# A convolution-attention kernel: the last 18 keys scored once per image, two map tiles in turn, a 1 KB ring of DMA descriptors

## The chip, the cores and the metric

The kernel runs on one core of one Trainium2 chip. Its time is the device time in microseconds (us), the median of several runs. A core has a matrix engine (TensorE, PE in the profile), a vector engine (VectorE, DVE), a scalar engine for activations (ScalarE, ACT), GpSimd (POOL), SyncE (SP), which only issues transfers, and 16 DMA engines. PE's results go to PSUM, where the kernel's tiles take eight banks of 128 partitions by 512 fp32 numbers; its other tiles are in SBUF. All data here is fp32.

## What is computed

The input is `x`, eight images of 256 channels by 32 by 32 pixels. Layer 0 is attention in eight heads of 32 channels, with a query for each of the 1024 pixels. Its keys and values come from four pooled copies of the projected map, 32x32, 16x16, 11x11 and 5x5, each with a depthwise 3x3 convolution added, so there are 1024 + 256 + 121 + 25 = 1426 keys. Layer 1 is attention over the 1024 tokens of an image with one head of 256, and a mixture of eight three-layer networks (the FFN) follows it. Cut to what matters here:

```python
kv = jnp.einsum('bchw,oc->bohw', x, kv_w)
k_map, v_map = kv[:, :C], kv[:, C:]
def pooled(t):                       # ratios 1, 2, 3, 6
    p = jnp.einsum('bchw,ph,qw->bcpq', t, Mh, Mw)
    p = p + _depthwise(p, dconv_w[i], dconv_b[i])
    ...
ks_ = _layernorm(pooled(k_map).transpose(0, 2, 1), norm_w, norm_b)
vs_ = _layernorm(pooled(v_map).transpose(0, 2, 1), norm_w, norm_b)
attn = jax.nn.softmax(jnp.einsum('bhqd,bhkd->bhqk', q_g, k) * SCALE, axis=-1)
out_att = jnp.einsum('bhqk,bhkd->bhqd', attn, v)
```

## The kernel before

**Units and steps.** Layer 0's attention runs in units: an image `b`, a half `c` of the heads (four heads, 32 partitions each) and a half of the queries (512). There are 8 x 2 x 2 = 32 units. The keys are cut in `NKC` = 12 chunks, eleven of 128 and a last one of 1426 - 11 x 128 = 18. A step takes one chunk in one unit, so the loop at L1827 has 384 steps. A step does the following.

- `scores` (L1477): for each of the four heads a product with 32 rows (the head's channels), up to 128 columns (the keys) and 512 moving elements (the queries). Each head has its own 32 rows of the array and its own PSUM bank of the tile `sc`, which is four banks and exists once. One activation then takes exp of all four banks, 128 x 2048 numbers, into a tile `pt`, of which there are six. The last chunk fills 18 partitions only, over the same 2048 numbers.
- `values` (L1487), one step later: four products with the keys as rows and the 32 channels of a head as columns, each into its own 32 partitions of the bank `pv`, added up over the twelve chunks.
- The softmax sums: after every second chunk `add` (L1499) has POOL issue a DMA that adds the newer `pt` onto the older one in SBUF. For the last chunk it adds 18 partitions. `sums` (L1506) adds the six resulting tiles of a unit on VectorE, and a product with ones sums over partitions.

So the products of `scores` use the array in strips of 32 rows, those of `values` in strips of 32 columns, and the rest of the program in one piece or, where `narrow` (L751) says so, in column strips.

**The order.** A planner, class `Flow` (from L656 on), writes the order of every engine's instructions at build time. It has a model of costs (`cost`, L721, and `note`, L761) and a list of generators. Before an instruction is recorded a generator yields what it needs (an engine, tiles that must be ready, a PSUM slot, or a condition `until`). In the gaps of the loop at L1827 `step` (L864) takes up runnable generators as filler: preparing the next image, then layer 1 of earlier images, by rank and with a budget of 4 us (`PACE`) and 2 us (`PACE1`) of PE time per step. `finish` runs generators until a condition holds, such as the next image's keys being there. The order is fixed in the program, and waits on semaphores guard the data.

**Maps.** For each image after the first, `maps` (L1088) projects four maps (two halves of values, then two of keys), each in three slices of up to 512 columns, from PSUM through ScalarE into `p` and into an accumulator `acc` (three of these). `convolve` (L1241) then runs the taps on VectorE (`taps`, L1215). There is one tile `p` (`pmap`, L1128). So a map's first two slices wait until the large taps of the previous map have read it (`read[0] >= len(todo)`), its last slice until all its taps are done, and the number of maps started is held by `len(todo) < 3 + 2 * freed[0]`. The first image (`first_maps`, L1144) uses a slot of `acc` as the `p` of its map 3. `by_tokens` (L1266) transposes finished maps to one key per partition and normalises them; `value_tokens` (L1433) keeps the results as `vts[b][g]`, four chunks in each.

**Descriptors.** [...] whose size can be given where the program is made (L2539); here it is left at its default.

Of the kernel before, what the change touches and what calls it, by code (L numbers as in the profile page):

```python
# [10 lines left out]
AF = mybir.ActivationFunctionType  # L11
# [5 lines left out]
P = 128  # L17
# [5 lines left out]
OFFS = (0, 1024, 1280, 1401)  # L23
NK = 1426
NKC = 12
NE = 8
SCALE0 = DH ** -0.5
SCALE1 = C ** -0.5
# [627 lines left out]
class Flow:  # L656
# [64 lines left out]
    def cost(self, engine, op, out, ins):  # L721
        n = 1
        for s in (out.shape if op != "bn_stats" else ins[0].shape)[1:]:
            n *= s
        if op == "tensor_reduce":
            n = 1
            for s in ins[0].shape[1:]:
                n *= s
        if "dma" in op:
            return 1.0 if engine == "POOL" else 0.4  # L730
        if engine == "PE":
            if op == "transpose":
                return 0.13
            c = max(0.2, 0.00169 * n)
            return c if self.tiling(ins) is None else c / 4
        psum = any(i.space == PSUM for i in ins)
        if engine == "ACT":
            return 0.15 + 0.00084 * n + 0.16 * any(i.free_size() == 1 for i in ins[1:])
        if engine == "POOL":
            if n <= 64 and op == "tensor_tensor":  # L740
                return 0.3 + 0.17 * n if n <= NKC else 0.3
            return 0.15 + (0.0023 if op == "tensor_tensor" else 0.0015) * n
        if op == "scalar_tensor_tensor":
            return 0.23 + 0.00103 * n
        if op == "reciprocal":
            return 0.1 + 0.0064 * n
        if op in ("tensor_scalar", "tensor_copy") and not psum:
            return 0.14 + 0.00065 * n
        return 0.15 + 0.00107 * n
# [5 lines left out]
    @staticmethod  # L755
    def tiling(ins):

        rows, columns = ins[0].shape[0], ins[0].shape[-1]
        return "columns" if columns <= DH and rows > 8 else "rows" if rows == DH else None

    def note(self, engine, op, ins, args, kwargs):  # L761
# [22 lines left out]
        if engine == "PE":  # L784

            tiling = None if op == "transpose" else self.tiling(srcs)
            if tiling != self.tiled:
                cost += {None: 0.2, "rows": 0.2, "columns": 0.13}[tiling]
                self.tiled = tiling

        wide = [a for a in srcs if a.space != PSUM and a.free_size() > 4]
# [103 lines left out]
def attention(tc, kit, f, outer, ended, nb, consts, x, t1, t2, hn, bounds, vecs, q_t, kv_t, proj_t, gqk_t, wqk, wqkv, vecs1, w1_d, w1c, gate_d, wrc, vecs2, bnvec):  # L895
# [6 lines left out]
    with ExitStack() as ctx:  # L902
# [159 lines left out]
            f.ve.tensor_tensor(bias, ps[:, 0:2], vec[:, V_PB : V_PB + 2], ALU.add)  # L1062

        ks, qs, vts = {}, {}, {}
        made = [0]
        turn = [-1]
        todo, done, read, freed, key_parts, normalised = [], [], [4], [0], [0], [0]

        def pe(*tiles, tag=None):
            return "PE", tiles, tag  # L1070
# [7 lines left out]
        def pool(*tiles):  # L1078
            return "POOL", tiles, None

        def until(cond):
            return None, cond, None

# [4 lines left out]
        def maps(xp):  # L1088

            for m in (2, 3, 0, 1):  # L1090
                c = m % 2
                yield until(lambda: read[0] >= len(todo) and len(todo) < 3 + 2 * freed[0])
                p = pmap
                acc = T(work, [P, NK], "acc", bufs=3)
                for s0, w in KEY_SLICES:
                    if s0 >= HW:
                        yield until(lambda: len(done) >= len(todo))
                    src = source(xp, s0, w)
                    yield pe(src, tag="sm")
                    ps = small()  # L1100
                    for k in range(2):
                        f.pe.matmul(
                            ps[:, :w],
                            lhsT=kvw[:, k, m * P : (m + 1) * P],
                            rhs=src[:, k, :],
                            start=k == 0,
                            stop=k == 1,
                        )
                    f.act.activation(p[:, s0 : s0 + w], ps[:, :w], AF.Copy)
                    for s, n in enumerate(SIDES):  # L1110
                        a, z = max(OFFS[s], s0), min(OFFS[s] + n * n, s0 + w)
                        if a < z:
                            f.act.activation(
                                acc[:, a:z],
                                ps[:, a - s0 : z - s0],
                                AF.Identity,
                                bias=db(c, s),
                                scale=mid[:, c * 4 + s : c * 4 + s + 1],
                            )
                todo.append((c, p, acc))  # L1120
# [4 lines left out]
            return dy, dx, max(0, -dy), n - max(0, dy), max(0, -dx), n - max(0, dx)  # L1125


        pmap = T(work, [P, NK], "p")  # L1128
        f.split(pmap, 512, HW)
        first, large, whole, pooled, asked = {}, [], [], [], []  # L1130

        def first_diagonals():
# [11 lines left out]
        def first_maps(xp):  # L1144


            for m in range(4):
                if m < 2:
                    p = T(work, [P, 4, 512], "pt", bufs=6).rearrange("p j q -> p (j q)")
                    acc = T(l1, [P, NK], "v") if m else T(work, [P, NK], "kn", bufs=3)  # L1150
                else:
                    p = T(work, [P, NK], "acc", bufs=3) if m == 3 else pmap
                    acc = T(work, [P, NK], "acc", bufs=3)
                for t in (p, acc):
                    if t is not pmap:
                        f.split(t, 512, HW)
                first[m] = p, acc
            for m, s0 in [(m, s0) for g in (0, 2) for s0 in (0, 512) for m in (g, g + 1)] + [(m, HW) for m in range(4)]:
# [70 lines left out]
        def first_taps():  # L1229
            for m in (2, 3):  # L1230
                yield until(lambda: "maps" in large)
                yield from taps(m - 2, 0, *first[m])
                large.append(("values", m))
            yield until(lambda: whole)
            for m in (2, 3, 0, 1):
                for s in range(1, 4):
                    yield from taps(m % 2, s, *first[m])
                whole.append(m)
            done.extend(first[m][1] for m in (2, 3, 0, 1))
# [193 lines left out]
        def value_tokens(b, g):  # L1433
# [2 lines left out]
            accs = done[4 * b : 4 * b + 2] if b else [first[m][1] for m in (2, 3)]  # L1436
            vt = T(work, [P, 4, C], "vt", bufs=6)
            yield from by_tokens(accs, vt, 4 * g)
            vts[b][g] = vt

        def key_tokens(b, g):
# [45 lines left out]
        def values(b, c, kc, pt, pv):  # L1487
            w = KEY_CHUNKS[kc][1]
            for j in range(4):
# [3 lines left out]
                    lhsT=vts[b][kc // 4][:w, kc % 4, h * DH : (h + 1) * DH],  # L1493
                    rhs=pt[:w, j, :],
                    start=kc == 0,
                    stop=kc == NKC - 1,
                )

        def add(kc, pt, into):  # L1499

# [323 lines left out]
        f.spawn(chain(mix(), weights1(), outputs()), 5)  # L1824
        f.spawn(layer1(), 6)
        f.columns = True
        steps = [(b, c, half, kc) for b in range(nb) for c in range(2) for half in range(2) for kc in range(NKC)]  # L1827

        pts = {}
        for i in range(len(steps) + 1):  # L1830
            if i < len(steps):
# [9 lines left out]
                    f.finish(lambda: {0, 1}.issubset(whole))  # L1841
                if b == 0 and kc == 0:
                    f.finish(lambda: (c, half) in asked)
                pts[i] = scores(b, c, sl, kc)
                f.step()
            if i:
                b1, c1, half1, kc1 = steps[i - 1]
                if kc1 == 0:
                    pv = T(psum, [P, 512], "pv")
                    pairs = []  # L1850
                    sl1 = slice(half1 * 512, half1 * 512 + 512)
                    f.spawn(unit(b1, c1, sl1, i // NKC, pairs), 0)
                f.finish(lambda: kc1 // 4 in vts[b1])
                values(b1, c1, kc1, pts[i - 1], pv)
                if kc1 % 2:
                    add(kc1, pts.pop(i - 1), pts[i - 2])
                    pairs.append(pts.pop(i - 2))
                if kc1 == NKC - 1:
                    f.finish(lambda: projected[0] >= b1)
                    f.act.activation(atts[b1, c1][:, sl1], pv, AF.Copy)  # L1860
            if i < len(steps):
# [688 lines left out]
```

## Time and profile before

| | us |
|---|---|
| median of 3 runs (3305.45 to 3312.34) | 3309.68 |
| the profiled execution's own time | 3310.0 |
| its span, from the first to the last instruction | 3308.1 |
| time outside the span (difference) | 1.9 |
| layer 0's attention loop, from its first exp at 84 to its last at 1956 | 1872 |
| after the loop (rest of layer 1, then the FFN) | 1352 |

The page gives each engine's busy time over the whole span. Since the parts of the program have different limits, the table of stretches matters more, with the span cut where an image's attention starts. Names in the rows are tiles: `sc`, `pv` and `pt` as above, `kn` a half of the keys, `q` the queries, `vt` values by token; `sm` and `sx` are the three PSUM banks of all filler. Nearly every instruction is recorded through one line (L669), so that groups are told apart by their tiles. "32*128" in a row of PE is rows by columns of the array in use. An fp32 product shows as two instructions, so four products are x8.

### The profile page before, as it was taken

The numbers are of one execution on the slowest core, as the hardware profiler recorded it, in microseconds if no ns is written. First come the engines' busy times: TensorE is split into PE (matmuls) and PEld (weight loads), VectorE is DVE, ScalarE is ACT, GpSimd is POOL, SyncE is SP. The second block draws the span as 40 slices with busy tenths as digits, with TensorE's granted clock in tenths as the row PEclk, the third lists the DMA queues.
The fourth block names the chain that finished last, engine by engine and source line by source line (L and its number), as shares of the span: only waits on it lengthen the run. The fifth ranks groups of instructions, "written<-read, shape, count | busy, mean of one in ns | idle before, by whom it ended". The sixth has DMA issues, their size and how long they took to land. (4 is left out here: it accounts for less than half of the span.)

```text
span 3308.1 us, 57168 instructions
## 1 busy us (share of the span) xinstructions
PE 3098.8 (94%) x23038; PEld 1790.7 (54%) x23038; DVE 2455.2 (74%) x4068; ACT 1733.4 (52%) x2330; POOL 1217.1 (37%) x1315
## 2 busy tenths in 40 slices
PE   8687899999999999999899889999999999999997
PEld 4322234334334334334334236767888888888886
DVE  5687688797886887987875455447888787777776
ACT  4476675675676576666666543343333344444442
POOL 2211411412213213213112112007656567777775
PEclk9798999999999999999999999999999999999999
DMA  2357655745646756655556557125434310000000
GB/s 75 84 127 165 131 100 145 147 93 143 142 103 143 147 132 131 132 133 114 125 127 143 122 119 246 60 86 178 153 134 153 139 65 20 20 25 27 20 14 21
DMA packets 110754, 362.70 MB, mean 110 GB/s; under 512 B 13504, under 2 KB 38856, under 8 KB 87248
## 3 DMA queue, kind: packets, MB, share of 16 engines
q0 software_dynamic: 28608, 179.85, 28.2%
q1 hardware_dynamic: 78512, 177.13, 15.5%
q8 instruction: 184, 3.01, 0.4%
q10 hardware_dynamic: 3360, 1.97, 0.2%
q14 instruction: 90, 0.74, 0.1%
HBM read 112.45 MB, written 81.31 MB: 59 GB/s over the span
## 5 line engine op out<-in xcount | busy, mean ns | idle before, releaser
L669 ACT ACTIVATE pt<-sc 128x2048 f32<-128x2048 f32 (+1 forms) x384 | 720.5, 1876 | 298.5 <-PE sc L669 246.5
L669 DVE SCALAR_TENSOR_TENSOR acc<-p,vec,acc 128x225 f32<-128x225 f32 (+7 forms) x928 | 532.7, 580 | 31.3 <-ACT acc L669 6.5
L669 PE MATMUL sc<-q,kn 32*128 32x512 f32 (+1 forms) x3072 | 448.1, 653 | 108.0 <-ACT pt L669 105.8
L669 DVE TENSOR_TENSOR pt<-pt,pt 128x1024 f32<-128x1024 f32 x320 | 384.4, 1244 | 144.3 <-DMA pt<-pt 133.1
L669 POOL DMA_DIRECT2D pt<-pt x192 | 171.4, 894 | 769.3 <-ACT pt L669 592.9
L669 PE MATMUL pv<-pt,vt 128*32 128x512 f32 (+1 forms) x3072 | 420.2, 620 | 0.0
L669 ACT ACTIVATE p1c<-bank 128x256 f32<-128x256 f32 x230 | 87.9, 382 | 565.9 <-PE bank L669 554.3
L669 ACT ACTIVATE h<-h,bnvec 128x512 f32<-128x512 f32 x460 | 348.0, 805 | 63.8 <-DVE h L669 54.7
L669 POOL TENSOR_TENSOR rstd<-rstd,mhalf 128x4 f32<-128x4 f32 (+2 forms) x88 | 108.8, 1237 | 697.7 <-DVE rstd L669 586.3
L669 DVE TENSOR_TENSOR h<-p1c,bank 128x512 f32<-128x512 f32 x230 | 156.7, 681 | 211.6 <-PE bank L669 211.0
L669 PEld LDWEIGHTS sc<-q,kn 32*128 32x128 f32 (+1 forms) x3072 | 116.8, 179 | 320.2 <-ACT pt L669 217.8
L669 POOL TENSOR_TENSOR tm<-h,tm 128x256 f32<-128x256 f32 x210 | 241.8, 1151 | 16.5
L669 DVE TENSOR_TENSOR h<-u,bank 128x256 f32<-128x256 f32 x460 | 234.3, 550 | 7.9
L669 PEld LDWEIGHTS pv<-pt,vt 128*32 128x32 f32 (+1 forms) x3072 | 60.9, 108 | 304.2 <-issue 295.1
L669 POOL TENSOR_TENSOR tm<-h 128x512 f32<-128x512 f32 x105 | 137.9, 1313 | 195.2 <-ACT h L669 194.1
L669 DVE TENSOR_TENSOR h<-h,gate 128x1024 f32<-128x1024 f32 x128 | 203.2, 1588 | 0.5 <-ACT h L669 0.5
L669 PE MATMUL bank<-h,w2e 128*128 128x256 f32 (+1 forms) x604 | 193.3, 448 | 2.8 <-DVE h L669 1.9
L669 PE MATMUL sm<-p,v 128*32 128x256 f32 (+1 forms) x2416 | 192.3, 379 | 0.7 <-ACT p L669 0.7
L669 PE MATMUL y<-t,s3e 128*128 128x256 f32 x768 | 187.0, 379 | 2.2 <-POOL t L669 2.1
L669 PE MATMUL bank<-t,s1e 128*128 128x256 f32 x750 | 183.8, 381 | 3.5 <-DVE h L669 3.5
L669 POOL TENSOR_TENSOR t<-h,t 128x256 f32<-128x256 f32 x216 | 172.9, 800 | 17.0
L669 POOL TENSOR_TENSOR t<-h 128x512 f32<-128x512 f32 x108 | 140.1, 1298 | 105.4 <-DVE h L669 80.0
(315 smaller groups left out, 5448.6 us busy)
## 6 DMA issues: line engine op xcount, KB each, us to landing
pt<-pt POOLq DMA_DIRECT2D x160, 1024.0 KB, 7.5
h<-h SPq DMA_DIRECT2D x118, 512.0 KB, 3.3
xi<-in_x_dram SPq DMA_DIRECT2D x16, 512.0 KB, 6.7
t<-t SPq DMA_DIRECT2D x8, 1024.0 KB, 5.6
res<-t SPq DMA_DIRECT2D x32, 256.0 KB, 4.7
t<-res SPq DMA_DIRECT2D x32, 256.0 KB, 4.6
hn<-res SPq DMA_DIRECT2D x32, 256.0 KB, 4.2
hn<-hn SPq DMA_DIRECT2D x16, 512.0 KB, 4.4
```

Source lines behind the costliest of these rows:

```text
L669: ins = fn(*args, **kwargs)
```

## The change

- The last chunk leaves the step list for three of an image's four units. In the first unit (`c` = 0, `half` = 0), after chunk 7, `tail_scores` makes the scores of the last 32 keys for all four units of the image: sixteen products of 32 rows by 32 columns by 512, product (`u`, `j`) with the rows of head `j` and into the partitions 32`u` of bank `j`. One exp puts them into `ptail`. The loop has 8 x (4 x 11 + 1) = 360 steps.
- Of these 32 keys the first 14 are also in chunk 10. `tail_values`, called in each unit right after the values of chunk 10, takes the 32 rows of its unit from `ptail` and a value tile `vz` that holds zeros for those 14 keys. `vz` (two tiles, by the image's parity, zeroed once on POOL) is filled by four small transfers on SP per image, at the end of `value_tokens` for the last group. `tail_add` adds the 18 rows of `ptail` onto chunk 10's `pt` by a DMA from POOL.
- Two tiles `p` are used in turn, so that `maps` may be one map further ahead (`len(todo) - 1`), and the first map of the second image may be projected before any tile of the first is freed.
- The planner's model gets the price of the new kind of product, and the descriptor ring has 1024 bytes of each partition.

```diff
-        todo, done, read, freed, key_parts, normalised = [], [], [4], [0], [0], [0]
+        todo, done, read, freed, key_parts, normalised = [], [], [2], [0], [0], [0]
...
-                yield until(lambda: read[0] >= len(todo) and len(todo) < 3 + 2 * freed[0])
-                p = pmap
+                yield until(
+                    lambda: read[0] >= len(todo) - 1 and len(todo) < (3 + 2 * max(freed[0], 2) if freed[0] else 5)
+                )
+                p = pmaps[len(todo) % 2]
...
-                        yield until(lambda: len(done) >= len(todo))
+                        yield until(lambda: len(done) >= len(todo) - 1)
...
+            if g == 2:
+                yield sp(vt)
+                for u in range(4):
+                    c = u // 2
+                    f.sp.dma_start(vz[b % 2][DH * (u + 1) - NT : DH * (u + 1), :], vt[:NT, 3, c * P : (c + 1) * P])
...
+        def tail_scores(b):
+            t = T(psum, [P, 4, 512], "sc")
+            for j in range(4):
+                r = slice(DH * j, DH * j + DH)
+                for u in range(4):
+                    c, half = divmod(u, 2)
+                    f.pe.matmul(
+                        t[DH * u : DH * u + DH, j, :],
+                        lhsT=ks[b, c][r, NK - DH :],
+                        rhs=qs[b, c][r, half * 512 : half * 512 + 512],
+                        start=True,
+                        stop=True,
+                    )
+            f.act.activation(ptail, t, AF.Exp, scale=SCALE0)
+
+        def tail_values(b, u, pv):
+            for j in range(4):
+                f.pe.matmul(
+                    pv[DH * j : DH * j + DH, :],
+                    lhsT=vz[b % 2][DH * u : DH * u + DH, DH * j : DH * j + DH],
+                    rhs=ptail[DH * u : DH * u + DH, j, :],
+                    start=False,
+                    stop=True,
+                )
+
+        def tail_add(u, into):
+            rows = slice(DH * (u + 1) - NT, DH * (u + 1))
+            f.pool.dma_start(
+                out=into[:NT].rearrange("p j q -> p (j q)"),
+                in_=ptail[rows].rearrange("p j q -> p (j q)"),
+                accum_op=ALU.add,
+            )
...
-        steps = [(b, c, half, kc) for b in range(nb) for c in range(2) for half in range(2) for kc in range(NKC)]
+        order = [*range(8), NKC - 1, *range(8, NKC - 1)]
+        steps = [
+            (b, c, half, kc)
+            for b in range(nb)
+            for c in range(2)
+            for half in range(2)
+            for kc in order
+            if kc < NKC - 1 or c + half == 0
+        ]
...
-                pts[i] = scores(b, c, sl, kc)
+                if kc == NKC - 1:
+                    f.finish(lambda: key_parts[0] > 3 * b + 2 and (b, 1) in qs and (b or len(asked) == 4))
+                    tail_scores(b)
+                else:
+                    pts[i] = scores(b, c, sl, kc)
...
-                if kc1 == NKC - 1:
+                if kc1 == NKC - 2:
+                    u = 2 * c1 + half1
+                    tail_values(b1, u, pv)
+                    pairs.append(pts.pop(i - 1))
+                    tail_add(u, pairs[-1])
...
-    nc = _bacc.Bacc("TRN2", target_bir_lowering=False, num_devices=1)
+    nc = _bacc.Bacc("TRN2", target_bir_lowering=False, num_devices=1, dynamic_dma_scratch_size=1024)
```

## Prediction

> **What bounds the kernel.** I read the busy times by stretch first, because the page's averages mix an attention loop with an FFN. The stretches are the eight images' turns in the loop (two of them left out), the end of layer 1 and the FFN. Columns: stretch, its length, busy time of PE, PEld, DVE, ACT and POOL with instruction counts, granted clock, DMA share, GB/s.
>
> ```profile
> 84.00:326.00 242.00, 181.95 (x1367) 64.33 (x1370) 185.54 (x382) 146.60 (x171) 45.60 (x55) 0.89 0.56 125
> 326.00:563.00 237.00, 217.04 (x2090) 79.04 (x2083) 183.53 (x317) 154.70 (x186) 58.18 (x68) 0.95 0.60 129
> ...
> 1042.00:1271.00 229.00, 217.64 (x2224) 83.29 (x2220) 193.75 (x329) 152.21 (x185) 58.42 (x65) 0.99 0.62 135
> ...
> 1746.00:1956.00 210.00, 198.85 (x2140) 76.24 (x2140) 103.31 (x143) 124.64 (x128) 38.59 (x44) 0.98 0.64 130
> 1956.00:2010.00 54.00, 40.40 (x152) 23.34 (x144) 18.73 (x21) 10.90 (x21) 14.47 (x33) 0.87 0.62 213
> 2010.00:2240.00 230.00, 229.15 (x896) 163.06 (x895) 114.90 (x210) 86.16 (x147) 17.22 (x23) 0.99 0.31 109
> ```
>
> PE is at 95% in a middle image (217.64 of 229) and at 99.6% after the loop, while DVE stays below 85% and ACT below 68%. So PE bounds the program, and its idle time adds to the end. Only the first image, which has no layer 1 to fill gaps, has PE at 75%. PE's own rows come next, by shape, with exp's two rows (busy us, mean ns of one, idle before).
>
> ```profile
> L669 PE MATMUL sc<-q,kn 32*128 32x512 f32 x2816 | 413.7, 657 | 93.6 <-ACT pt L669 91.5 <-ACT kn L669 0.8
> L669 PE MATMUL pv<-pt,vt 18*32 18x512 f32 x256 | 34.9, 616 | 0.0
> L669 PE MATMUL sc<-q,kn 32*18 32x512 f32 x256 | 34.4, 607 | 14.3 <-ACT pt L669 14.3
> L669 ACT ACTIVATE pt<-sc 128x2048 f32<-128x2048 f32 x352 | 660.8, 1877 | 276.6 <-PE sc L669 225.8 <-DMA pt<-pt 24.7 <-issue 10.1
> L669 ACT ACTIVATE pt<-sc 18x2048 f32<-18x2048 f32 x32 | 59.7, 1866 | 21.9 <-PE sc L669 20.7 <-issue 1.2
> ```
>
> The last chunk's 18 keys cost as much as 128: 34.4 / 32 = 1.075 us of PE per step for scores and 1.866 us of ACT. Last, the order in time on PE in three steps of image 4.
>
> ```profile
> 1121.05 1.14 PE L669 MATMUL sc<-q,kn 32*128 32x512 f32 x8
> 1122.12 1.06 PE L669 MATMUL pv<-pt,vt 128*32 128x512 f32 x8
> 1123.12 0.66 PE L669 MATMUL sm<-con,t 128*128 128x128 f32 x4
> 1124.19 1.14 PE L669 MATMUL sc<-q,kn 32*128 32x512 f32 x8 [0.42 <-ACT pt L669]
> ...
> 1128.46 1.06 PE L669 MATMUL pv<-pt,vt 128*32 128x512 f32 x8
> 1129.35 1.90 PE L669 MATMUL sm<-xi,kvw 128*32 128x512 f32 x16
> ```
>
> A step with little filler lasts 3.14 us (1121.05 to 1124.19). The next scores need the one `sc` tile, so they wait for exp, and PE has about 2 us for `values` and filler. A step with more filler lasts as long as its PE work. Such waits are 93.6 + 14.3 = 107.9 us by the rows, 105.8 of it for exp.
>
> **The sum, part by part.**
>
> *Scores, removed:* 32 groups at 1.075 = **34.4 us** of PE.
>
> *Scores, added:* 8 groups of sixteen products, each on its own 32x32 block. The trace shows neither blocks nor sixteen at once. Its nearest rows are four side by side in row strips (`sc`) and in column strips (`pv`), and both take one group's time. In the group at 1124.19 the first four starts lie 7 ns apart. By the row, a group is 1.07 + 24 more instructions x 0.007 = 1.24 us. [...] The ends are 1.07, all free, and 4 x 1.07 = 4.3, if the four products that share a strip of rows queue. I take 1.24, since strips of either kind do run side by side here: **9.9 us**.
>
> *A rule against the change:* [...] here a new mode comes in. In the trace `pv` followed by work in its own mode takes 0.89 us (1128.46 to 1129.35), before another mode 1.00 (1122.12 to 1123.12), and `sc` before `pv` 1.07. So a change of mode costs 0.11 to 0.18 us. Two steps before had filler, sc, pv, filler, sc, pv, filler: four changes. Now they have filler, sc, pv, tail values, filler: again four. The removed group's 1.075 thus holds about 0.15 that comes back behind chunk 10, in 24 places: **+3.6 us**. If the row's saving stood whole it would be 0; if each of 32 tail values paid two changes of its own, 32 x 0.36 = 11.5.
>
> *Values of the last keys:* as many groups, 32 rows in place of 18, in the same 512-element stream: 34.9 us before and after, 0.
>
> PE's work: -34.4 + 9.9 + 3.6 = **-20.9 us**.
>
> *Waits for exp:* 24 exps go, 24 x 1.87 = 44.9 us of ACT, which does not bound. What counts is PE's idle time before scores, 105.8 / 384 = 0.275 us a step. The order of the changed program's PE queue has about as many loop gaps with under 0.8 us of filler as before (72 to 74), so the waits thin out only with the steps: 24 x 0.275 = **-6.6 us**. Ends: 0, if all wait just as long elsewhere; 24 x 0.447 = 10.7 by the removed row's own idle.
>
> *Filler left behind:* 24 budgets fewer move about 70 us of layer 1 past the loop, counted in that order at 0.46 us per 256 columns. It lands where PE is busy 229.15 of 230 us, so 0. Without that cover, at the loop's 95%, it would cost 3.5.
>
> *Two map tiles:* DVE's tap row waits 31.3 us in all over 928 taps, and DVE is not the bound, so 0. Upside: the second image's first map can fill some of the first image's 60 idle us of PE (242 - 182), at most 5. Downside: its taps delay the first image's keys by as much.
>
> *Moved and added on queues:* SP gets 32 transfers of 18 rows of 512 B. The issue waits for ACT to normalise value chunk 11; behind it in SP's order stand filler loads and stores (`res`, `hn`, `q`, the weights). Values are made before keys, so tail values come many steps later, and a transfer lands in 3 to 5 us by rows such as `hn<-pool` at 3.2. I take 0, at most 1 us for each of 8 images. On POOL the two memsets lie in the start, and accumulating transfers stay 192. The new wait of the sixteen scores is for all keys of the image and both `q`. Chunk 8 already waited for the keys, one step later, and `q` is fetched as the unit begins, over 25 us earlier. Nothing on ACT stands behind it but exp: 0. `ptail` frees `pt` slots (exp waits 24.7 us for them now), which I leave for the upside.
>
> *Ring of 1 KB:* Two rows bear on it.
>
> ```profile
> q0 software_dynamic: 28608, 179.85, 28.2%
> pt<-pt POOLq DMA_DIRECT2D x160, 1024.0 KB, 7.5
> ```
>
> 28608 packets over 192 + 28 transfers and 16 engines are 8 per engine and transfer. A transfer lands in 7.5 us and they are issued every second step (6.3 us at the least), so two or three are under way. [...] so 0.
>
> **Sum:** 3308.1 - 20.9 - 6.6 = 3280.6, with 1.9 outside **3282.5**. The profiled execution (3310.0) is 0.3 over the median shown, so I say **3282 us**, 0.8% less. A measurement of this kernel tells about 0.2% (7 us) from no change.
>
> **Rivals.**
>
> 1. *Each removed step takes its whole period along* (3262, chance 0.17). In the unit with the least filler of each image, and in the first image, steps last 3.1 us and the moved values hide under exp. Ten of the 24 places would then give 3.14 and not 1.2, some 20 us more. For it: units of 45 to 50 us in every image, close to 12 x 3.14 = 38. Against it: filler pushed out must be done elsewhere.
> 2. *Half is given back* (3296, 0.13). A shorter loop lets DVE fall behind with the keys (193.75 of 229 in a middle image), and PE waits at the image's start. For it: 60 idle us in the first image. Against it: in `finish` the planner fills with layer 1.
> 3. *The sixteen products queue in four rounds* (3307, 0.07): 8 x 4.3 = 34.4 takes back all the scores gave, then +3.6 - 6.6. No change that can be told. Against it: four different streams already run at once in `pv`.
> 4. *The ring holds POOL, slower* (3335, 0.06). If each accumulating DMA could only be written once the last had drained, POOL would be held 7.5 us in place of 0.9 by 188 transfers, 1240 us more in a loop of 1872 where it is busy some 440. Then `pt` slots and the small powers on POOL come late. At 0.16 us of PE per transfer the gain is gone; at 0.3 it is 56 us. Against it: the packet count above.
>
> The forecast has 0.55; 0.02 remains for other cases of the planner's order. **Range** 3256 to 3301: it takes in the first two rivals and the bounds of the modes, the waits and the maps. Faster by over 0.2%: forecast, rivals 1 and 2, 0.86; within: 0.07; slower: 0.07.
>
> **What would show it.** Scores of 32*32 in about 1.2 us per group (4.3: rival 3). PE busy near 3078 us. Idle before `sc` on exp near 99. Units 2 to 4 of an image shorter by 1.2 us each (3: rival 1). POOL's issue of `pt<-pt` still at 894 ns (several us: rival 4). The stretch after the loop as dense but some 70 us longer. I am wrong if PE's busy time falls by 20 and the span does not.

## The result, and the profile after

| | before | changed |
|---|---|---|
| median of 12 runs each, on one chip (us) | 3310.87 | 3297.39 |
| ratio, with its 95% interval | 1 | 0.9962 [0.9952, 0.9973] |
| span of the profiled execution (us) | 3308.1 | 3298.6 |
| PE busy (us) | 3098.8 | 3093.2 |
| PE idle, span less busy (us) | 209.3 | 205.4 |
| attention loop, first exp to last (us) | 1872 | 1795 |
| after the loop (us) | 1352 | 1421 |

The change gains 13 us where 28 were forecast. The stretches of the changed kernel come first (columns as in the prediction: stretch, length, busy time of PE, PEld, DVE, ACT and POOL, granted clock, DMA share, GB/s). The rows are the first two images, a middle one, the last, the first 52 us after the loop, and a part of the FFN.

```profile
83.00:322.00 239.00, 186.77 (x1390) 67.36 (x1388) 186.01 (x399) 144.92 (x174) 50.62 (x60) 0.89 0.55 124
322.00:527.00 205.00, 184.40 (x1668) 65.59 (x1668) 181.17 (x303) 144.23 (x172) 66.47 (x75) 1.00 0.67 143
988.00:1221.00 233.00, 215.65 (x2174) 82.75 (x2170) 188.86 (x330) 146.35 (x182) 51.56 (x60) 0.97 0.63 136
1689.00:1878.00 189.00, 182.72 (x2052) 67.81 (x2056) 97.07 (x123) 111.20 (x104) 33.75 (x38) 0.99 0.68 139
1878.00:1930.00 52.00, 35.45 (x133) 18.16 (x126) 24.79 (x37) 8.26 (x16) 16.95 (x37) 0.90 0.70 222
1930.00:2160.00 230.00, 226.07 (x887) 164.26 (x886) 108.41 (x191) 83.48 (x145) 15.82 (x16) 1.00 0.30 103
```

The loop is shorter by 77 us and what follows it longer by 69. PE still bounds both parts: 92.6% in the middle image, 98.3% in the FFN. Next, groups of PE by shape (count, busy us and mean ns of one, idle before and what ended it) of the changed kernel.

```profile
L670 PE MATMUL sc<-q,kn 32*128 32x512 f32 x2816 | 414.6, 659 | 106.7 <-ACT pt L670 104.0 <-ACT kn L670 1.0 <-ACT ptail L670 0.5
...
L670 PE MATMUL bank<-h,w2e 128*128 128x512 f32 x248 | 114.9, 606 | 3.4 <-ACT h L670 3.4
L670 PE MATMUL bank<-h,w2e 128*128 128x256 f32 x388 | 100.6, 380 | 2.5 <-DVE h L670 2.5
...
L670 PE MATMUL pv<-ptail,vz 32*32 32x512 f32 x256 | 35.7, 629 | 0.0
...
L670 PE MATMUL sc<-q,kn 32*32 32x512 f32 x256 | 10.7, 656 | 1.0 <-ACT pt L670 1.0
```

The new scores take 10.7 us for eight groups and replace a row of 34.4. In the order of time (start, duration, group, idle before) the first of these eight groups, the second, and one of the removed groups in the kernel before, each with what PE starts next:

```profile
156.64 2.67 PE L670 MATMUL sc<-q,kn 32*32 32x512 f32 x32
159.25 1.93 PE L670 MATMUL pv<-pt,vt 128*32 128x512 f32 x8
...
360.63 1.16 PE L670 MATMUL sc<-q,kn 32*32 32x512 f32 x32
361.71 1.07 PE L670 MATMUL pv<-pt,vt 128*32 128x512 f32 x8
```

```profile
378.42 1.05 PE L669 MATMUL sc<-q,kn 32*18 32x512 f32 x8 [1.09 <-ACT pt L669]
379.40 1.07 PE L669 MATMUL pv<-pt,vt 128*32 128x512 f32 x8
```

From its start to PE's next, the second group takes 1.08 us, and the first, where the granted clock was 0.50, takes 2.61. The removed group takes 0.98, less than the 1.075 that its row's busy time gives, because the end of a group overlaps the start of the next. Idle time before `sc` on exp was 91.5 + 14.3 before; it is 104.0 + 1.0 now. The same view of the kernel before has, for the FFN's second layers:

```profile
L669 PE MATMUL bank<-h,w2e 128*128 128x256 f32 x420 | 108.6, 380 | 1.9 <-DVE h L669 1.9
L669 PE MATMUL bank<-h,w2e 128*128 128x512 f32 x184 | 84.7, 604 | 0.8 <-ACT h L669 0.8
```

The row of 512 columns grew from 184 instructions to 248, which is 8 blocks of eight (four products) each. This is the direct form of a second layer, one of two that the program has (see below). Last, POOL's row of the accumulating transfers and, from the list of DMA issues, their landing time in the changed kernel:

```profile
L670 POOL DMA_DIRECT2D pt<-pt x160 | 147.2, 920 | 565.7 <-ACT pt L670 399.2
...
pt<-pt POOLq DMA_DIRECT2D x160, 1024.0 KB, 7.9
```

An issue takes 920 ns (894 before) and a transfer 7.9 us (7.5). The small ring does not hold POOL.

**A measure used from here on.** The trace records, from some 16 to 20 us into the span on, when the clock granted to PE was 0.5. In the changed kernel a group of `values` took 1.83 us from its start to PE's next where the clock was 0.5 (at 91.24 in the last section), and 1.00 at full clock (at 94.51). So half of PE's busy time in these windows is counted as lost to the clock ("half-clock loss"). Busy time less this loss is PE's work at full clock. The span is then work + loss + idle:

| | work at full clock | half-clock loss | idle | span |
|---|---|---|---|---|
| before | 3050.7 | 48.2 | 209.3 | 3308.1 |
| changed | 3037.8 | 55.4 | 205.4 | 3298.6 |
| difference | -12.9 | +7.2 | -3.9 | -9.5 |

Each line is one profiled execution, and not all of it can be read equally well. `ring_alone` (below) has the PE order of the kernel before, instruction for instruction. Its execution has nearly the same work (3050.4), but a loss of 54.0 and an idle time of 197.1. So work can be compared between single executions, while a difference of 6 us in loss or of 12 us in idle time needs no other order of PE.

For the clock there is more on record, since every execution comes with its mean granted clock. The span times the share that was not granted is called "taken by the clock" here; it counts idle time too, so it is larger than the loss. Over 56 executions of the kernel before its mean is 67.9 us (clock 0.9795; 68 to 72 us on the five chips used here), over the 12 of the changed kernel 68.4 (0.9793), and single executions scatter by about 5 us around such means. So the clock takes as much from the changed kernel as from the one before, and the +7.2 is what these two executions drew. By the medians the change gains 13.5 us: 12.9 of work, and 0.6 of idle time and clock together.

### The profile page after: what moved, and what is told of

Read it like the earlier page. It is cut to its first block, busy times and chain, and to the rows that moved or that the text cites. A ratio compares the mean times of both kernels' runs of the same rounds, so it can differ in the third digit from the quotient of the medians.

```text
span 3298.6 us, 55657 instructions
## 1 busy us (share of the span) xinstructions
PE 3093.2 (94%) x22264; PEld 1793.6 (54%) x22264; DVE 2466.9 (75%) x4060; ACT 1692.0 (51%) x2298; POOL 1174.7 (36%) x1269
## 4 chain that ended last, share of the span: by engine, by line
PE 46%; DVE 4%; DMA 1%; ACT 1%; issue 1%; POOL 1%; SPq 0%; DVEq 0%; ACTq 0%; POOLq 0%
PE bank L670 21%; PE y L670 10%; PE sm L670 9%; PE sc L670 3%; PE pv L670 2%; PE sx L670 2%; DVE h L670 1%; DVE u L670 1%; DVE c L670 1%; ACT pt L670 1%; DVE t L670 0%; DMA pt<-pt 0%; DMA t<-t 0%; POOL t L670 0%; ACT h L670 0%
## 5 line engine op out<-in xcount | busy, mean ns | idle before, releaser
L670 ACT ACTIVATE pt<-sc 128x2048 f32<-128x2048 f32 x352 | 660.8, 1877 | 291.4 <-PE sc L670 226.4
L670 DVE SCALAR_TENSOR_TENSOR acc<-p,vec,acc 128x961 f32<-128x961 f32 (+3 forms) x960 | 565.0, 597 | 32.5 <-ACT acc L670 6.2
L670 PE MATMUL sc<-q,kn 32*128 32x512 f32 (+1 forms) x3072 | 425.4, 659 | 107.7 <-ACT pt L670 105.0
L670 PE MATMUL pv<-pt,vt 128*32 128x512 f32 x2816 | 387.0, 622 | 0.0
L670 POOL DMA_DIRECT2D pt<-pt x160 | 147.2, 920 | 565.7 <-ACT pt L670 399.2
L670 DVE TENSOR_TENSOR h<-u,bank 128x256 f32<-128x256 f32 (+1 forms) x444 | 226.1, 550 | 7.6
L670 POOL TENSOR_TENSOR tm<-h,tm 128x256 f32<-128x256 f32 x194 | 220.4, 1136 | 15.2
L670 PE MATMUL bank<-h,w2e 128*128 128x256 f32 (+1 forms) x636 | 215.6, 468 | 6.0 <-ACT h L670 3.4
L670 PEld LDWEIGHTS pv<-pt,vt 128*32 128x32 f32 x2816 | 56.1, 109 | 277.8 <-issue 264.8
L670 PE MATMUL sm<-y,t 128*32 128x256 f32 (+1 forms) x1872 | 178.7, 379 | 0.6 <-DVE st L670 0.6
```

Source lines behind the costliest of these rows:

```text
L670: ins = fn(*args, **kwargs)
```

## The experiments

Ratios are to the kernel before on the same chip, with 95% intervals. In the expectations L says that filler which leaves the loop costs more after it; M and E that the maps' rule (its longer lead, or its earlier start) costs; O that the planner's order as a whole draws more or less idle and half-clock time.

### The parts one by one

`ring_alone` is the kernel before with the 1 KB ring; PE's order is the same. `maps_alone` adds to that the two map tiles and their rules. `tail_alone` is the changed kernel with one map tile and the old rules.

```diff
 ring_alone, maps_alone: before with
+    dynamic_dma_scratch_size=1024
 maps_alone too; tail_alone the reverse, on the changed kernel:
-                yield until(lambda: read[0] >= len(todo) and len(todo) < 3 + 2 * freed[0])
-                p = pmap
+                yield until(
+                    lambda: read[0] >= len(todo) - 1 and len(todo) < (3 + 2 * max(freed[0], 2) if freed[0] else 5)
+                )
+                p = pmaps[len(todo) % 2]
```

> The kernel before with nothing but the ring of 1 KB. Theory (the ring holds all that is under way): 3310.9, within 0.1%, POOL's issue of pt<-pt still near 894 ns. Rival (descriptor writing waits for the ring to drain, and this ate part of the gain): slower by 5 to 15 us, the issue clearly longer than 0.9 us.

> The kernel before with the ring and the two map tiles; the last chunk is scored in every unit as before. Theory (the maps only move filler about): 3305 to 3312, PE idle in the first image some 8 us less than the 60 of before, 25 second layers of the FFN in the direct form in place of 23, which costs 1.4. Rival 1 (the maps cost what is missing): 3318 or more. Rival 2 (the maps bring most of the 13 us and the tail little): 3300 or less.

> The changed kernel with one map tile as before. Theory (scores give 22, more mode changes take 6.6, waits give 4, the FFN takes 1.4 for 25 direct second layers in place of 31): 3292. Rival 1 (maps cost the missing part): 3283. Rival 2 (maps bring the gain): 3303 or more.

| | median us | ratio | work | half-clock loss | idle |
|---|---|---|---|---|---|
| ring_alone | 3303.4 | 0.9983 [0.9975, 0.9991] | 3050.4 | 54.0 | 197.1 |
| maps_alone | 3318.4 | 1.0027 [1.0020, 1.0035] | 3052.0 | 60.9 | 205.0 |
| tail_alone | 3280.7 | 0.9920 [0.9905, 0.9934] | 3037.2 | 36.4 | 201.1 |

The ring costs nothing. The tail by itself gives 29 us, close to the forecast for the whole, and the maps take some of it back both with the tail (16.7 us) and without (15, beside `ring_alone`). So the maps looked guilty. But their work at full clock is the same as without them within 1.6 us; what differs is the clock and the idle time. Over all executions the clock took 65.1 us in `ring_alone` and 76.4 in `maps_alone`, 57.4 in `tail_alone` and 68.4 in the changed kernel: 11 us more with the maps in both cases.

### Fewer second layers in the direct form

While layer 1's rest is still filler, the FFN's `experts` runs blocks ahead of it, and their second layers take four products of 512 columns (eight instructions, the first of the two rows in the changed kernel) where all others take seven of 256. A block in the direct form costs about 0.54 us more of PE: counted from each start to PE's next, the groups of the second layers took 5.2 us more for 8 more such blocks, 4.3 with the half-clock loss taken out. `staged23` limits them.

```diff
-NSTAGED = 64
+NSTAGED = 23
```

> The changed kernel with NSTAGED = 23 in place of 64: 26 second layers of the FFN are direct in place of 31, the attention loop has the same order. Theory (each direct second layer costs PE 0.7 us more than the other form, and this is a part of what is missing): 3.5 us less than the changed kernel's 3297.4, so 3294, PE busy 3.5 less. Rival (the direct blocks fill time that layer 1's chain would leave idle): 3297 or more, with the idle time after the loop grown by 3 or more.

3310.9 us, 1.0007 [1.0000, 1.0014]: slower than the changed kernel, not faster. There were 26 direct blocks for 31, and work fell by 2.3 us, about as it should (5 x 0.54 = 2.7); but idle time rose by 11.5 (205.4 to 216.9), all of it after the loop (45.2 to 57.9), and over its 22 executions the clock took 77.6 us in place of 68.4. So it seems that the blocks had filled a place where little else could run.

### Which half of the maps' rule, and how much filler

`no_early` and `early_only` each keep one half of the new rule; `tail_less_filler` and `tail_more_filler` are `tail_alone` with another filler budget per step.

```diff
 no_early, on the changed kernel:
-    lambda: read[0] >= len(todo) - 1 and len(todo) < (3 + 2 * max(freed[0], 2) if freed[0] else 5)
+    lambda: read[0] >= len(todo) - 1 and len(todo) < 3 + 2 * freed[0]
 early_only, on the changed kernel:
-    lambda: read[0] >= len(todo) - 1 and len(todo) < (3 + 2 * max(freed[0], 2) if freed[0] else 5)
+    lambda: read[0] >= len(todo) and len(todo) < (3 + 2 * max(freed[0], 2) if freed[0] else 5)
-    yield until(lambda: len(done) >= len(todo) - 1)
+    yield until(lambda: len(done) >= len(todo))
 tail_less_filler (1.8), tail_more_filler (2.4), on tail_alone:
-PACE1 = 2.0
+PACE1 = 1.8
```

> The changed kernel with two map tiles and the look-ahead of one map, but with the old limit on maps started, so that the second image's first map is not made early. Theory L (what costs is filler that leaves the attention loop: by the order, loop filler is 946 in the planner-free count where the changed kernel has 931 and the one-tile kernel 978): 3291, PE idle before sc on exp above 105. Theory M (the look-ahead itself, through VectorE and ScalarE getting two maps' work in a burst, is what costs): 3297, like the changed kernel. Theory E (the early first map costs): 3281.

> The changed kernel with two map tiles and the early first map, but each map waits for the one before as in the old kernel. Loop filler by the order is 963. Theory L: 3286. Theory M (look-ahead costs): 3281. Theory E (the early first map costs): 3297.

> One map tile as in tail_alone, and PACE1 = 1.8 in place of 2.0, which alone takes loop filler from 978 to 947 and leaves 27 direct second layers in place of 25. Nothing of the maps differs. Theory L: 3291 to 3293, half-clock time up, exp waits up by 5 or more. Theories M and E: 3282, for two direct layers cost 1.4.

> One map tile, PACE1 = 2.4: loop filler 1015 in place of 978, 23 direct second layers. Theory L: 3268 to 3275, exp waits down. Theories M and E: 3279.

| | median us | ratio | work | half-clock loss | idle |
|---|---|---|---|---|---|
| no_early | 3272.8 | 0.9886 [0.9871, 0.9901] | 3037.3 | 38.5 | 193.9 |
| early_only | 3275.5 | 0.9890 [0.9875, 0.9905] | 3033.9 | 39.3 | 205.5 |
| tail_less_filler | 3276.0 | 0.9892 [0.9877, 0.9907] | 3031.2 | 49.3 | 195.1 |
| tail_more_filler | 3338.2 | 1.0085 [1.0071, 1.0099] | 3034.2 | 57.9 | 243.5 |

Each half of the maps' rule is fast with the tail, and only both together are slow. That leaves neither M nor E. L falls too: less filler in the loop made the kernel no slower, and more of it made it 57 us slower, through idle time (201.1 to 243.5) and half clock (36.4 to 57.9). What all share is their work: 3031 to 3038 us with the tail, 3050 to 3052 without.

One difference between two of these orders can be read directly. In the order of time on PE, this is the end of the loop in the changed kernel:

```profile
1905.01 0.59 PE L670 MATMUL sm<-diag,con 128*128 128x256 f32 x2
1915.98 5.22 PE L670 MATMUL bank<-hn,w1e 128*128 128x512 f32 x8 [10.38 <-DMA hn<-hn]
1921.04 0.60 PE L670 MATMUL sm<-con,t 128*128 128x128 f32 x4
1921.48 3.60 PE L670 MATMUL bank<-hn,w1e 128*128 128x512 f32 x8
```

And this in `no_early`:

```profile
1908.38 10.52 PE L670 MATMUL sm<-y,t 128*128 128x256 f32 x48
1919.67 7.11 PE L670 MATMUL bank<-hn,w1e 128*128 128x512 f32 x16 [0.77 <-DMA hn<-hn]
```

In the changed kernel little of the last image's layer 1 was left to run in that place, and PE stood idle for 10.38 us until the FFN's first input had landed. In `no_early` layer 1's products still filled it. And the first x8 after the pause took 5.22 us, the next x8 of the same kind 3.60. The stretches of the changed kernel there, by the same columns as above, show why:

```profile
1905.00:1910.00 5.00, 0.60 (x3) 0.19 (x1) 2.02 (x4) 0.00 (x0) 0.00 (x0) 0.89 0.64 253
1910.00:1916.00 6.00, 0.01 (x1) 0.05 (x1) 0.13 (x1) 0.00 (x0) 1.73 (x4) 0.50 0.69 207
1916.00:1919.00 3.00, 3.00 (x4) 1.45 (x5) 1.41 (x3) 0.00 (x0) 1.40 (x4) 0.50 1.01 356
1919.00:1922.00 3.00, 3.00 (x11) 1.44 (x11) 0.32 (x1) 1.53 (x2) 2.84 (x7) 0.98 1.03 387
```

The granted clock fell to 0.50 in the pause and stayed there for some 3 us of full work. This pause was thus paid twice: 10.38 us idle, and about half of the 3 us.

### The same change in other orders

If the gain depends on the order that the planner happens to find, it must be measured in more than one. `MARGIN` (1.5) is how long before `sc` comes free a filler's inputs must be ready for it to be taken; another value gives another order of the same work. `tail_rows128` tests the modes instead: on `tail_alone`, the tail values take all 128 rows, with zeros for the other units, and so use the array as `values` do, in 128 rows by 32 columns. "Mode" stands for the rows by columns in use: 128*32 here, 32*32 for the tail values otherwise.

```diff
-MARGIN = 1.5
+MARGIN = 1.6
 tail_rows128, on tail_alone (vz is one tile per unit, zero outside the unit's rows):
-                    lhsT=vz[b % 2][DH * u : DH * u + DH, DH * j : DH * j + DH],
-                    rhs=ptail[DH * u : DH * u + DH, j, :],
+                    lhsT=vz[b % 2][u][:, DH * j : DH * j + DH],
+                    rhs=ptail[:, j, :],
```

> The changed kernel with the planner's MARGIN 1.4 in place of 1.5: the same instructions of the tail and the maps, another order of filler (939 in the loop in place of 931, 28 direct second layers in place of 31). Theory O (no part of the change costs; the changed kernel drew a poor order): anywhere from 3265 to 3290, clearly under 3297 in this run or in that with 1.6. Theory M2 (look-ahead and early map together cost, whatever the order): 3293 to 3301 in both.

> The changed kernel with MARGIN 1.6: loop filler 942, 27 direct second layers. Theory O: 3265 to 3290 in this run or in that with 1.4. Theory M2: 3293 to 3301 in both.

> The kernel before with MARGIN 1.6, 23 direct second layers as before. It tells how far an order alone moves the kernel without the change. Theory O: within 15 us of 3310 on either side, not within 3. If it lands under 3290, the gain of the tail itself is in doubt; at 3307 to 3313 orders of the old kernel hardly matter.

> One map tile as in tail_alone; the values of the last keys are taken over all 128 rows of ptail, with a value tile per unit that holds zeros in the other units' rows, so that chunk 10's products and these share one mode (128 rows by 32 columns). By the rows, pv of both kinds took 374 us in tail_alone. If the extra changes of mode cost, it falls to 368 or less, and the time to 3275 if the order of the rest matters little. [...]

> The kernel before with MARGIN 1.4, the partner of after_margin_14 (3297.5). Theory O (the change takes some 20 us of PE work and waits off in the mean, and each order adds its own draw of half-clock time and idle time, 10 to 15 us either way): anywhere from 3290 to 3325; PE busy without half-clock loss near 3050. Theory M2 (the change as it stands brings 13 with every setting): 3310.

> The kernel before with MARGIN 1.7. Theory O: 3290 to 3325, and the pair's difference to after_margin_17 differs from 13 by 10 or more in one of the new pairs. PE busy without half-clock loss near 3050.

> The changed kernel with MARGIN 1.7: loop filler 934 and 32 direct second layers, almost the counts of the changed kernel itself. Theory O: 3265 to 3305; PE busy without half-clock loss near 3037. If the count of filler in the loop and of direct layers were the cause, it must come out at 3297 to 3300.

> The changed kernel with MARGIN 1.3: loop filler 931 like the changed kernel, 28 direct second layers. Theory O: 3265 to 3305; PE busy without half-clock loss near 3036. If loop filler were the cause: 3295 to 3299.

| MARGIN | before | ratio | changed | ratio | gain us |
|---|---|---|---|---|---|
| 1.3 | | | 3294.6 | 0.9953 [0.9933, 0.9973] | |
| 1.4 | 3321.2 | 1.0030 [1.0018, 1.0042] | 3297.5 | 0.9960 [0.9946, 0.9975] | 23.7 |
| 1.5 | 3310.9 | 1 | 3297.4 | 0.9962 [0.9952, 0.9973] | 13.5 |
| 1.6 | 3293.3 | 0.9951 [0.9936, 0.9965] | 3271.5 | 0.9887 [0.9871, 0.9903] | 21.8 |
| 1.7 | 3320.6 | 1.0036 [1.0026, 1.0047] | 3291.7 | 0.9934 [0.9911, 0.9957] | 28.9 |

The mean gain of the four pairs is 22.0 us, and the pair of the change itself is the least of them. Work at full clock falls in every pair, by 17.5, 12.9, 18.4 and 18.4 us (16.8 in the mean), so that 5.2 us are left for idle time and clock in the mean. Two kernels of a pair share the constant and not the order, so a single pair says little. One constant of the planner, which changes none of the computation, moves either kernel by 26 us and more. `after_margin_16` and `no_early` are the fastest versions measured, 1.1% faster than before and faster than the changed kernel.

`tail_rows128` took 3294.0 us, 0.9952 [0.9938, 0.9966], in an order that drew more half clock (54.9 us beside 36.4 in `tail_alone`). Its work says more than its time. The two kinds of `pv` follow each other like this in the changed kernel:

```profile
1878.33 1.04 PE L670 MATMUL pv<-pt,vt 128*32 128x512 f32 x8
1879.30 1.06 PE L670 MATMUL pv<-ptail,vz 32*32 32x512 f32 x8
```

The values of chunk 10 take 0.97 us there until the tail values start, against 0.89 before work in their own mode (in the prediction). In all, time from each start in `pv` to PE's next start (without waits) was 374.3 us in `tail_alone` and 371.8 in `tail_rows128`. With the half-clock loss taken out these are 365.2 and 358.3. By the same count it is 360.6 in the kernel before and 364.4 in the changed one, 359.8 to 361.8 in all orders without the tail and 362.5 to 365.6 in all whose tail has its own mode (no zeros added). So PE took about 4 us more for `pv` with the tail in its own mode, and no more than before with the tail in the mode of `values` (358.3 beside 360.6).

### Filling the pauses

That half clock follows pauses was up to here read from traces in which the order changed too. `zeros_alone` is the changed kernel, and `no_early_zeros` is `no_early`, with PE's order kept. Only where the planner saw `sc` come free over 0.51 us later, they add four products with zero weights to `pv` (79 and 83 groups).

```diff
+                gap = f.free("sc") - f.now["PE"]
+                if i and steps[i - 1][3] < NKC - 2 and gap > 0.51:
+                    n = min(512, int((gap - 0.2) / 0.00169))
+                    for j in range(4):
+                        f.pe.matmul(pv[DH * j : DH * j + DH, :n], lhsT=zero, rhs=qs[b1, c1][:, :n], start=False, stop=False)
```

> The changed kernel with work added in the pauses for exp: where the planner sees over 0.51 us until the sc tile comes free, four products with zero weights go into pv (79 groups, up to 512 columns each, 77 us of PE by the 1.06 us of a values group; nothing else in PE's order changes, and pv gains zeros). Theory G, half clock follows stretches in which PE is thinly busy: the half-clock loss falls from 55.4 us to 35 or less, most of it in the first image; PE busy rises by some 50 (77 added, over 20 of loss gone), idle falls by 55 to 70, and the time falls by 5 to 20 us. Theory T, the clock takes its own course: the loss stays at 50 to 60 and the time is the same, or up to 20 us longer where a group of zeros outlasts its pause.

> The same in the kernel with the old limit on maps (83 groups of zero products, 82 us of PE; order otherwise as in no_early, which took 0.9886 of before with a half-clock loss of 38.5 us). Theory G: the loss falls to 25 or less and the time by 5 to 12 us, to about 0.986. Theory T: the loss stays at 36 to 42 and the time is the same or up to 20 us longer.

| | median us | ratio | work | half-clock loss | idle | span |
|---|---|---|---|---|---|---|
| changed | 3297.4 | 0.9962 [0.9952, 0.9973] | 3037.8 | 55.4 | 205.4 | 3298.6 |
| zeros_alone | 3291.7 | 0.9944 [0.9929, 0.9960] | 3100.7 | 46.2 | 148.7 | 3295.6 |
| no_early | 3272.8 | 0.9886 [0.9871, 0.9901] | 3037.3 | 38.5 | 193.9 | 3269.7 |
| no_early_zeros | 3274.7 | 0.9890 [0.9874, 0.9906] | 3105.0 | 27.0 | 134.7 | 3266.7 |

The first image of the changed kernel, by stretch, and then the same 238 us of `zeros_alone`:

```profile
84.00:322.00 238.00, 185.77 (x1380) 66.36 (x1379) 185.12 (x395) 143.92 (x174) 50.62 (x60) 0.89 0.55 124
```

```profile
84.00:322.00 238.00, 207.73 (x1661) 75.31 (x1660) 187.43 (x396) 149.72 (x181) 55.62 (x69) 0.93 0.58 130
```

The granted clock rises from 0.89 to 0.93. The loss there falls by 9.7 us (22.3 to 12.6), which is all that the whole kernel's falls by (9.2). In `no_early_zeros` the loss falls by 11.5 us. Over all executions the clock took 68.4 us in the changed kernel and 55.4 in `zeros_alone` (6), 55.6 in `no_early` (4) and 45.8 in `no_early_zeros` (5). So with the order unchanged, filling the pauses raised the clock in both kernels. The sizes were over-forecast (20 and 13 us), and no time can be told to be gained: the zero products need 63 and 68 us of PE, the pauses they fill are 57 and 59, and what the clock returns pays for the rest (62.9 - 56.7 - 9.2 = -3.0).

## Why the prediction was right and wrong

**Right.** The mechanism of the main term stands: sixteen products on 32x32 blocks ran side by side, and the rival of four rounds (4.3) is refuted. In the changed kernel seven of the eight groups take 1.07 to 1.09 us from their start to PE's next, as a group of four does (1.07). So the 24 more instructions, priced at 7 ns each, cost next to nothing; the prediction had this only as an end of the term ("1.07, all free"). The mean of all eight is 1.27 (10.2 / 8), because the first image's group took 2.61 at a granted clock of 0.50; that this lies beside the forecast 1.24 is luck. The term of the modes stands too: `pv` rose by 3.8 us at full clock (360.6 to 364.4), forecast 3.6. The ring rival is refuted by `ring_alone` (0.9983) and by the row of 920 ns; how much a ring of 1 KB can hold, no trace shows. Filler moved past the loop lengthened that part by 69 us, forecast 70. The two map tiles cost PE hardly any work of their own (`maps_alone` 3052.0, `ring_alone` 3050.4).

**The first step that failed** is "the waits thin out only with the steps", -6.6, with the assumption under it: that the changed order draws as much idle time per step as the old one, and as much time at half clock, for which the sum had no term at all. Idle time and clock together gave 0.6 us by the medians. Idle time on exp stayed (105.8 to 105.0, by the rows of `sc`) although 24 exps went. Between orders of nearly equal work, idle time runs from 190 to 244 us and the loss from 36 to 61 (no zeros added). That is more than the whole forecast, and a forecast from one order's averages could not know which would be drawn. As a mean over orders the step was not far off, 5.2 us in the four pairs. Its own reason, that about as many gaps had little filler, counted gaps and not how long and how close together they were.

**The second is "It lands where PE is busy 229.15 of 230 us, so 0".** What landed after the loop did so densely, but it kept layer 1 unfinished for longer, so 8 more blocks took the dearer form of a second layer: +4.3 us of PE's work. I had looked at how busy the place was, and not at what else the program decides by it.

**One term was mis-sized.** The removed scores were put at their row's busy time, 34.4 us. From each start to PE's next they took 32.2, and 31.3 with the half-clock loss taken out; the new ones took 8.9 by that count. So the scores gave 22.4 us, where 24.5 were forecast.

Together this closes the gap between 27.5 forecast and 13.5 measured, 14.0 us. PE's work fell by 12.9 for 20.9. Of the missing 8.0, 4.3 are direct second layers, 2.1 the scores, 0.2 the modes, and 1.4 the runs don't assign. The other 6.0 are the waits and the clock, 0.6 for 6.6.

**The rivals.** The time lies near rival 2 (3296), but not by its way. PE did not wait for late keys at an image's start, since idle time before `sc` on `kn` is 1.0 us in the row above. The half was given back by the FFN's form, by the price of the scores and by waits that did not thin out. That is a case I did not have. Rival 1 (3262) did not come, although its sign did: units 2 to 4 of an image last 51.0 us in the mean, from one first exp to the next, and lasted 55.0. The sign could not tell it from the forecast, whose 70 us of moved filler alone make 2.9 us for each of the 24 removed steps.

**What stays open.** Why exactly this order draws more than its neighbours. The counts that I tried (direct blocks, filler left, idle at the loop's end) don't fix the time: `after_margin_17` has 32 direct blocks and is no slower than the changed kernel with 31 (3291.7 beside 3297.4). Whether both map rules together cost something in most orders is not settled either. Four of the five settings of `MARGIN` with both take 3291.7 to 3297.5, and one takes 3271.5; with the tail and at most one of the rules, four of six kernels take 3272.8 to 3280.7, but these were run at one `MARGIN` only. `ring_alone` is 0.17% faster than before in an order of PE that is the same; I have no cause for that.

## What to carry to other kernels

Where a planner places filler between dependent steps, as here, a removed piece of work may be worth its own PE time only in the mean over orders; try the change under three or four values of a harmless planner constant, before and after, and compare the pairs. Put a term for the granted clock into the sum (36 to 61 us here), and look for stretches in which PE is thinly busy: in these traces 91% of the 3.4 us pieces behind one with under 30% of work, and 45% behind one with 30 to 60%, ran at half clock (table below). When work moves past a boundary, ask which decisions of the program hang on where it ends. Price a group of products from its start to PE's next start and with the clock in view, and don't read a few us of idle time or clock out of one profiled execution.

## What was not expected of the hardware

The clock granted to PE is 1.0 or 0.5 in these traces, nothing between, in windows of mostly 3.4 us or multiples of it. The changed kernel's trace has 23 windows at 0.5: twelve of 3.41 us, six of 6.83, two of 10.24, two of 17.07, and one of 9.38 in which the record ends. The kernel before has 21, thirteen of them of 3.41 us. In the changed kernel's first image it reads like this (order of time on PE):

```profile
84.79 1.14 PE L670 MATMUL sc<-q,kn 32*128 32x512 f32 x8
85.86 1.07 PE L670 MATMUL pv<-pt,vt 128*32 128x512 f32 x8
89.36 1.94 PE L670 MATMUL sc<-q,kn 32*128 32x512 f32 x8 [2.44 <-ACT pt L670]
91.24 1.90 PE L670 MATMUL pv<-pt,vt 128*32 128x512 f32 x8
93.07 0.44 PE L670 MATMUL sm<-p,res 128*128 128x64 f32 x2
93.44 1.14 PE L670 MATMUL sc<-q,kn 32*128 32x512 f32 x8
94.51 1.07 PE L670 MATMUL pv<-pt,vt 128*32 128x512 f32 x8
95.51 0.55 PE L670 MATMUL sm<-con,kt 128*128 128x128 f32 x3
```

After one pause of 2.44 us the next group of scores takes 1.94 us instead of 1.14. The granted clock is 1.00 over the first two groups (84.79 to 86.93), 0.50 from 89.57 to 92.98, and 1.00 behind that, where the next such pair (at 93.44) takes 1.14 and 1.07 again. Over the traces of all 20 kernels, cut into pieces of 3.413 us (those before the clock's record begins are left out; a piece counts as half clock when most of it was):

```
PE busy in the piece before     pieces    of them at half clock
under 30%                          297    91%
30 to 60%                          436    45%
60 to 90%                         2151     9%
90% and more                     16303     0.6%
```

So in these traces half clock goes with little work on PE just before it (91% of the pieces beside 0.6%). In `zeros_alone` products with zero weights counted as such work: the first image's granted clock rose from 0.89 to 0.93. How the chip sets the clock, no trace shows. What half clock cost in kernels whose PE is 93 to 94% busy was the surprise: 36 to 61 us of 3300 in the profiled executions (no zeros added).
